# A selective-scan block on five engines: one more state's drive moved to TensorE, four of them by diagonal matrices

## The chip, the cores and the metric

One core of a Trainium2 chip runs the whole program. The metric is the device time of one execution in microseconds (us), as the median of several runs. TensorE (PE, with its weight loads PEld), VectorE (DVE), ScalarE (ACT), GpSimd (POOL) and the DMA queue of SyncE (SP) run their own instruction streams in order and wait for each other on semaphores.

## The reference

Two layers follow each other; each normalises its input over groups of 4 channels (32 groups, mean and variance over all positions) and adds its result to its input. The input is 16 images of 64 x 64 positions with 128 channels, in fp32. Layer 0 is a two-dimensional recurrent cell over rows and columns, which the change does not touch except through the shared normalisation function. Layer 1 is a bidirectional selective scan (Mamba) over the 4096 tokens of an image:

```python
def _mamba(x, in_w, conv_w, conv_b, x_w, dt_w, dt_b, A_log, D, out_w):
    xc, z = jnp.split(x @ in_w.T, 2, axis=-1)             # 256 channels each
    xc = silu(causal_conv(xc, conv_w, 4 taps) + conv_b)
    dt, Bm, Cm = jnp.split(xc @ x_w.T, [8, 8 + 16], axis=-1)
    dt = softplus(dt @ dt_w.T + dt_b)
    dA = jnp.exp(dt[..., None] * -jnp.exp(A_log))         # per channel and state
    dBx = dt[..., None] * Bm[:, :, None, :] * xc[..., None]
    h = dA_t * h + dBx_t ;  y = sum over 16 states of h * C_t
    y = (y + xc * D) * silu(z)
    return y @ out_w.T
y_fwd = _mamba(x);  y_bwd = flip(_mamba(flip(x)));  x + y_fwd + y_bwd
```

The weights are the same in both directions, so the two scans' sums can be added before the gate `silu(z)` and the output projection.

## The kernel before

Layer 1 works on an image in 16 **passes**: 8 chunks of 512 tokens forwards (the first half; passes 0 to 7), then the same 8 chunks backwards (the second half; passes 8 to 15). Channels lie on partitions in two halves (h = 0, 1) of 128, tokens on the free axis. Every pass computes for each of the 16 states s: the decay exp(dt * A) on ACT (L919), the **drive** dt * xc * B, the scan h = decay * h + drive on DVE (L952, one instruction of 128x512 for each half), the product with C, and the sum over states, which PE makes by transposing each product into an accumulating PSUM tile `py` (`sums`, L987, 8 transposes of 128x128 a state; the tile has tokens on partitions).

The states are of three kinds, and the kind says which engine does the two products:

- **plain** (7 states: 0, 6, 7, 8, 10, 12, 15): the drive on POOL (L924, `dtx` times a row of B that a DMA spread over the 128 partitions into `br`), the product with C on POOL (L978, with a row of C spread into `cr`). The decay goes into a PSUM bank.
- **mixed** (5 states: 2, 4, 5, 11, 14): the drive is made with tokens on partitions, where B is a scalar of each partition: ACT multiplies the transposed `dtxt` by it (`drive_turned`, L931, 4 instructions of 128x256), and PE transposes the result back into two PSUM banks (`drive_back`, L939, 8 transposes). The product with C stays on POOL.
- **turned** (4 states: 1, 3, 9, 13): the drive as in mixed; the scan writes in place in PSUM, the product with C is on DVE (L980), and DVE also copies the carried column (L967).

POOL makes `dtx` = dt * xc as well (L893), once a pass. Around the states stand, on PE: the convolution folded with the input projection (L801, 8 matmuls of 128x512), `xproj` (L838), `dtproj` (L876), the transposes of `dtx` (L900) and of the B columns (L858), `skip` (xc * D by a diagonal matrix into `py`, L987 with `ddiag`) and in the second half the gate's projection (L821). ACT takes most of these out of PSUM and applies silu and softplus, with three table loads a pass.

At the end of a pass, `finish`: in the first half ACT copies `py` to `yf` (L1014); in the second half DVE adds `yf` to `py` (L1017) and multiplies by the gate z into `y` (L1018). Then PE transposes `y` (`back`, L1024), ACT takes it (L1031), PE projects it with `out_wT` (`project`, L1041, 2 matmuls of 512 columns, channels on partitions), ACT copies that (`project_take`, L1052), PE transposes it to tokens on partitions (`store`, L1057, 4 transposes), and DVE adds it to the residual (L1063), which a DMA writes out.

During the first half of an image's passes the next image is read, transposed (L758), copied by ACT (L766), and its statistics are taken by DVE (L767). Then `normal` turns the statistics into scale and shift: `group_norm` averages by a matmul with `gavg` (L493), copies the mean to SBUF (L495), and DVE computes the deviation, its square and the sum with the variances (L497, L499, L500) before a second matmul (L502) and the root on ACT (L504).

The **order of the work** is not the program's nesting. `order_of_issue` lists every operation with its inputs, buffers, an assumed cost (`COST`) and an urgency (the tables `AT` and `STATE`, in units of one state); `simulate` plays them on five engines with those costs and writes down the order in which they begin. That order is fixed at build time, and each engine's queue executes its own part of it in order. `RINGS` gives the number of buffers of each kind: six PSUM banks for everything but `py` (two banks), 6 `br`, 5 `cr`, 3 `dbx`, 2 `dbt`, 3 `hst`, 4 `hc`.

```python
TURNED = (1, 3, 9, 13)
MIXED = (2, 4, 5, 11, 14)
...
# pool: plain drive                      # ACT + PE: mixed and turned drive
nc.gpsimd.tensor_mul(t, self.dtx, bc(self.brow.pop(s), 1, NH))
...
nc.scalar.activation(t[:, j, :], self.dtxt[:, j, :], AF.Copy, scale=self.bt[:, j, s : s + 1])
...
nc.tensor.transpose(t[:, j * P : (j + 1) * P], self.dbt[s][:, j, h * P : (h + 1) * P], ident)
```

Of the kernel before, what the change touches and what calls it, by code (L numbers as in the profile page):

```python
# [14 lines left out]
P = 128  # L15
# [17 lines left out]
TURNED = (1, 3, 9, 13)  # L33
MIXED = (2, 4, 5, 11, 14)
# [3 lines left out]
    "bank": 6, "py": 1, "das": 2, "dbx": 3, "dbt": 2, "hst": 3, "hc": 4,  # L38
    "br": 6, "cr": 5, "xc": 2, "dt": 2, "dtx": 2, "dtxt": 2, "dbl": 2, "bt": 2, "z": 1, "y": 1,
# [4 lines left out]
    "conv": 3.5, "gate": 0.9, "silu": 0.62, "softplus": 0.65, "gate_take": 0.6, "dtproj": 0.95,  # L44
    "xproj": 1.8, "xproj_take": 0.5, "bturn": 0.35, "bturn_take": 0.15, "times": 2.37,
    "turn": 0.55, "turn_take": 0.5, "decay": 0.62, "drive": 2.37, "drive_turned": 1.6,
    "drive_back": 0.52, "scan_turned": 1.28, "scan": 1.19, "keep_turned": 0.15, "keep": 0.1,
    "out_turned": 0.61, "out": 2.37, "sums": 1.0, "skip": 0.42, "finish": 1.0, "finish_last": 2.4,
    "back": 0.55, "back_take": 0.5, "project": 1.8, "project_take": 0.5, "store": 0.5,
    "store_take": 0.65, "residual": 0.1, "read_load": 0.1, "read_turn": 0.5, "read_take": 0.6,  # L50
    "normal": 5.0, "normalise": 0.75, "spread": 0.1, "rows": 0.1, "store_out": 0.1,
# [9 lines left out]
    "conv": -26.36,  # L61
    "gate": 4.72,
    "session": 9.0,
    "xproj": -16.72,
    "xproj_take": -15.49,
    "bturn": -16.32,
    "bturn_take": -19.05,
    "dtproj": -8.22,
    "times": -3.14,
    "turn": -1.06,  # L70
    "turn_take": -5.63,
    "skip": 5.5,
    "residual": 13.47,
    "finish": 17.28,
    "back": 19.53,
    "back_take": 20.1,
    "project": 21.46,
    "project_take": 24.04,
    "store": 24.79,
    "store_take": 25.37,  # L80
    "read_load": 1.91,
    "read_turn": 7.21,
    "read_take": 8.49,
    "normal": 2.71,
    "normalise": 1.36,
# [3 lines left out]
    "decay_turned": -0.91,  # L89
    "decay_mixed": -3.33,  # L90
    "decay_plain": -1.6,
    "drive_turned": -2.74,
    "drive_mixed": -2.49,
    "drive_back": 0.01,
    "drive": -2.5,
    "out_turned": -0.93,
    "out_mixed": 1.73,
    "out_plain": 2.27,
    "keep": -0.87,
    "sums_turned": 3.93,  # L100
    "sums_mixed": 4.73,
    "sums_plain": 6.15,
    "row_b": -6.28,
    "row_c": -4.0,
# [7 lines left out]
def order_of_issue(images):  # L112
# [5 lines left out]
    def tile_of(ring):  # L118
        tiles.append([ring, 0, None])
        return len(tiles) - 1  # L120
# [17 lines left out]
    for i in range(-2, n_pass):  # L138
# [83 lines left out]
        for s in range(NS):  # L222
# [23 lines left out]
            else:  # L246
                bt, bx = tile_of("dbt"), bank
                put("drive_turned", (s,), "ACT", at + s + STATE["drive_" + k],
                    after=[get(("turn_take", i, q)) for q in range(NB // 2)] + [get(("bturn_take", i))],
                    takes=[bt], uses=[T_["dtxt"], T_["bt"]], chain=("drive_turned", 0))  # L250
                for h in range(NH):
                    put("drive_back", (s, h), "PE", at + s + STATE["drive_back"] + 0.3 * h,
                        after=[get(("drive_turned", i, s))], takes=[bx[h]], uses=[bt],
                        chain=("bank", AHEAD))
                ready = [get(("drive_back", i, s, h)) for h in range(NH)]
            hh = bx if k == "turned" else [tile_of("hst")] * NH
            for h in range(NH):
                put("scan", (s, h), "DVE", at + s + 0.4 * h,
                    C_["scan_turned" if k == "turned" else "scan"],
# [11 lines left out]
            for h in range(NH if turned else 1):  # L271
                put("out_of", (s, h) if turned else (s,), "DVE" if turned else "POOL",
                    at + s + STATE["out_" + k] + 0.3 * h, C_["out_turned" if turned else "out"],
                    after=(scans[h : h + 1] if turned else scans) + [get(("spread", i, "c", s))],
# [11 lines left out]
        else:  # L286
            y, yt, xr = tile_of("y"), tile_of("yt"), tile_of("xr")
            put("finish", (), "DVE", at + AT["finish"], C_["finish_last"],
                after=adds + [("gate_take", i, NB // 2 - 1)], takes=[y], uses=[z])
            for h in range(NH):  # L290
# [5 lines left out]
            m, o = tile_of("misc"), tile_of("y")  # L296
            put("project", (), "PE", at + AT["project"],
                after=[get(("back_take", i, h)) for h in range(NH)], takes=[m, o], uses=[yt])
            put("project_take", (), "ACT", at + AT["project_take"], after=[get(("project", i))],
                uses=[m])  # L300
            m = tile_of("misc")
            put("store", (), "PE", at + AT["store"], after=[get(("project_take", i))], takes=[m],
                uses=[o])
            put("residual", (), "DMA", at + AT["residual"], takes=[xr])
            put("store_take", (), "DVE", at + AT["store_take"],
                after=[get(("store", i)), get(("residual", i))], uses=[m])
            put("store_out", (), "DMA", at + AT["store_take"], after=[get(("store_take", i))], uses=[xr])

        if b + 1 < images:
            if not second:  # L310
# [7 lines left out]
                    after=[get(("read_turn", b + 1, n))] + last, uses=[m])  # L318
            else:
                if n == NCH:  # L320
                    m = tile_of("misc")
                    put("normal", (), "DVE", at + AT["normal"], who=b + 1, key=("normal", b + 1),
                        after=[get(("read_take", b + 1, k)) for k in range(NCH)], takes=[m],
                        uses=[m])
# [140 lines left out]
def conv_preact_kernel(ctx: ExitStack, tc: tile.TileContext, a: dict):  # L465
# [23 lines left out]
    def group_norm(pool, psum, mv, n, tag, bank="misc"):  # L489


        pm = psum.tile([P, n], F32, name=f"pm_{tag}", tag=bank)
        nc.tensor.matmul(pm, lhsT=gavg, rhs=mv[:, :, 0], start=True, stop=True)  # L493
        mean = pool.tile([P, n], F32, name=f"mean_{tag}", tag="gn_mean")
        nc.vector.tensor_copy(mean, pm)  # L495
# [620 lines left out]
```

## Time and profile before

| what | value |
|---|---|
| median of 3 runs | 13995.0 us (13992.92 to 14003.99) |
| the profiled execution's own time | 13994.48 us |
| its span, first to last instruction | 13991.9 us |
| DVE busy | 12725.5 us, 15550 instructions |
| PE busy, PEld busy | 12411.7 us, 9345.3 us, 75020 instructions each |
| ACT busy | 12171.0 us, 22826 instructions |
| POOL busy | 12118.7 us, 5380 instructions |
| DMA | 1782.01 MB, mean 127 GB/s |

Layer 0 takes the first 1560 us or so of the span; layer 1, with 16 images of 16 passes, the rest. A group row gives line, engine, operation, the tiles (out<-in), shapes and count; then busy time, the mean length of one instruction in ns, and the idle time of the engine just ahead of them with what ended it. On PE, ACT and DVE the next instruction starts before the one ahead has ended, so the length of one (say 273 ns) is more than what a further one costs; that cost, called the **pitch** here, is the distance between starts in a timeline without idle time. A matmul of fp32 data appears as two records, a transpose as one. "Granted clock" (PEclk) is the share of full speed that TensorE was given.

### The profile page before, as it was taken

Reading aid. Unit: us, or ns where it says so; the run is one execution under the profiler, and the core shown is the slowest. Engines: PE = TensorE matmul, PEld = TensorE weight load, DVE = VectorE, ACT = ScalarE, POOL = GpSimd, SP = SyncE. Lnnn points to the kernel's source line nnn. Section 1 sums busy time; section 2 is a strip of 40 time slices with the busy share of each in tenths; the row PEclk is TensorE's granted clock in tenths of the full one; section 3 lists DMA queues with packets and bytes.
Section 4 is the critical chain, followed back from the end, with each engine's and each line's share of the span. In section 5 each row is a group of like instructions: output and inputs, shape, how many; then the busy total and the mean of one; then the engine's idle time right before and its main releaser. Section 6 shows DMA issues by size and latency. Waiting matters only on the chain. (4 is left out here: it accounts for less than half of the span.)

```text
span 13991.9 us, 233510 instructions
## 1 busy us (share of the span) xinstructions
PE 12411.7 (89%) x75020; PEld 9345.3 (67%) x75020; DVE 12725.5 (91%) x15550; ACT 12171.0 (87%) x22826; POOL 12118.7 (87%) x5380
## 2 busy tenths in 40 slices
PE   8999889898989888898989888888989898888988
PEld 7657766666666666666666666666666666666666
DVE  6777689999999999999999999999999999999998
ACT  2444699999999999999999999999999999999998
POOL 0111499999999999999999999999999999999998
PEclk7999899999999999999999999999999999999999
DMA  3221245444544545454545444454545444444544
GB/s 120 56 56 54 79 123 142 131 138 134 137 136 134 142 130 143 127 142 130 139 135 135 137 134 141 130 143 129 141 132 138 135 136 141 131 142 128 140 133 119
DMA packets 2060712, 1782.01 MB, mean 127 GB/s; under 512 B 959960, under 2 KB 1289184, under 8 KB 2059488
## 3 DMA queue, kind: packets, MB, share of 16 engines
q1 hardware_dynamic: 1981552, 1731.85, 44.2%
q10 hardware_dynamic: 77936, 35.23, 1.0%
q8 instruction: 598, 9.80, 0.3%
q14 instruction: 626, 5.13, 0.1%
HBM read 1679.37 MB, written 83.89 MB: 126 GB/s over the span
## 5 line engine op out<-in xcount | busy, mean ns | idle before, releaser
L978 POOL TENSOR_TENSOR hc<-hst,cr 128x1024 f32<-128x1024 f32 x3072 | 7228.5, 2373 | 448.0 <-DVE hst L952 245.7
L987 PE MATMUL py<-ident,hc 128*128 128x128 f32 x32768 | 4451.0, 283 | 565.8 <-POOL hc L978 449.2
L987 PEld LDWEIGHTS py<-ident,hc 128*128 128x128 f32 x32768 | 3822.0, 146 | 1328.3 <-POOL hc L978 761.1
L924 POOL TENSOR_TENSOR dbx<-dtx,br 128x1024 f32<-128x1024 f32 x1792 | 4239.8, 2377 | 1.8 <-POOL hc L978 0.4
L931 ACT ACTIVATE dbt<-dtxt,bt 128x256 f32<-128x256 f32 x9216 | 3858.4, 499 | 228.4 <-PE hps L939 226.8
L952 DVE TENSOR_TENSOR_SCAN hst<-da,carry,dbx 128x512 f32<-128x512 f32 x3136 | 3805.8, 1261 | 199.4 <-POOL dbx L924 126.6
L939 PE MATMUL hps<-ident,dbt 128*128 128x128 f32 x18432 | 2857.8, 288 | 306.8 <-ACT dbt L931 190.6
L919 ACT ACTIVATE das<-dt,A_log_sb 128x512 f32<-128x512 f32 x4608 | 3069.7, 713 | 67.3 <-DVE hps L952 43.6
L952 DVE TENSOR_TENSOR_SCAN hst<-das,carry,hps 128x512 f32<-128x512 f32 x2240 | 2727.8, 1262 | 145.8 <-issue 69.2
L939 PEld LDWEIGHTS hps<-ident,dbt 128*128 128x128 f32 x18432 | 2255.3, 148 | 731.5 <-ACT dbt L931 465.2
L919 ACT ACTIVATE da<-dt,A_log_sb 128x512 f32<-128x512 f32 x3584 | 2378.5, 682 | 106.6 <-DVE hst L952 78.4
L952 DVE TENSOR_TENSOR_SCAN hps<-das,carry,hps 128x512 f32<-128x512 f32 x1792 | 2201.4, 1269 | 149.8 <-PE hps L939 98.6
L801 PE MATMUL pp<-xT,wk 128*128 128x512 f32 x4096 | 1889.4, 604 | 120.2 <-DVE st L767 107.5
L980 DVE TENSOR_TENSOR hc<-hps,cr 128x512 f32<-128x512 f32 x2048 | 1389.7, 679 | 6.3 <-DMA cr<-rows 2.4
L621 POOL TENSOR_TENSOR a_f<-a_f,c 128x8 f32<-128x8 f32 (+31 forms) x254 | 200.0, 787 | 1354.6 <-ACT a_f L613 1179.1
L801 PEld LDWEIGHTS pp<-xT,wk 128*128 128x128 f32 x4096 | 748.5, 193 | 904.0 <-issue 765.0
L893 POOL TENSOR_TENSOR dtx<-dt,xc 128x1024 f32<-128x1024 f32 x256 | 608.1, 2376 | 52.4 <-DMA br<-rows 45.8
L876 PE MATMUL pv<-dbl,dt_wT 8*128 8x512 f32 x1024 | 530.6, 638 | 66.8 <-ACT xc L812 66.0
L952 DVE TENSOR_TENSOR_SCAN hst<-da,dbx 128x512 f32<-128x512 f32 x448 | 517.7, 1203 | 63.2 <-POOL dbx L924 53.9
L987 PEld LDWEIGHTS py<-ddiag,xc 128*128 128x128 f32 x4096 | 504.3, 192 | 59.1 <-issue 54.4
L987 PE MATMUL py<-ddiag,xc 128*128 128x128 f32 x4096 | 535.8, 275 | 2.7 <-ACT yf L1014 2.7
L838 PE MATMUL pd<-xc,x_wT_sb 128*40 128x512 f32 x1024 | 507.8, 620 | 0.0
(109 smaller groups left out, 11772.5 us busy)
## 6 DMA issues: line engine op xcount, KB each, us to landing
cr<-rows SPq DMA_DIRECT2D x4096, 256.0 KB
br<-rows SPq DMA_DIRECT2D x1792, 256.0 KB
carry<-hst SPq DMA_DIRECT2D x3072, 1.0 KB
xs<-in_x_dram SPq DMA_DIRECT2D x64, 512.0 KB
xl<-x SPq DMA_DIRECT2D x128, 256.0 KB
xr<-x SPq DMA_DIRECT2D x128, 256.0 KB
out_dram<-xr SPq DMA_DIRECT2D x128, 256.0 KB
xl<-in_x_dram SPq DMA_DIRECT2D x392, 64.0 KB
```

The source lines that it names most:

```text
L801: nc.tensor.matmul(pp, lhsT=wk[:, k, h * P : (h + 1) * P], rhs=xT[self.b % 2][:, t0 : t0 + T], start=(k == 0), stop=(k == TAPS - 1),)
L838: nc.tensor.matmul(pd, lhsT=x_wT[:, h, :], rhs=self.xc[:, h, :], start=(h == 0), stop=(h == NH - 1),)
L876: nc.tensor.matmul(pv, lhsT=dt_wT[:, h * P : (h + 1) * P], rhs=self.dbl[:RANK, :], start=True, stop=True,)
L893: nc.gpsimd.tensor_mul(self.dtx, self.dt, self.xc)
L919: nc.scalar.activation(t, self.dt[:, h, :], AF.Exp, scale=amat[:, h, s : s + 1])
L924: nc.gpsimd.tensor_mul(t, self.dtx, bc(self.brow.pop(s), 1, NH))
L931: nc.scalar.activation(t[:, j, :], self.dtxt[:, j, :], AF.Copy, scale=self.bt[:, j, s : s + 1])
L939: nc.tensor.transpose(t[:, j * P : (j + 1) * P], self.dbt[s][:, j, h * P : (h + 1) * P], ident)
L952: nc.vector.tensor_tensor_scan(t[:, self.rev], self.da.pop((s, h))[:, self.rev], dbx[:, self.rev], 0.0 if self.first else carry[:, self.d, ...
L978: nc.gpsimd.tensor_mul(self.hc[s], self.hst[s], bc(self.crow[s], 1, NH))
L980: nc.vector.tensor_mul(self.hc[s][:, h, :], self.h[s, h], self.crow[s])
L987: nc.tensor.matmul(self.py[:, j, h * P : (h + 1) * P], start=j // 2 not in self.banks, stop=self.added >= (NS + 1 - 1) * NB * NH, skip_gro ...
```

## The change

- **State kinds.** Plain states go from 7 to 6 (1, 6, 7, 10, 12, 15), mixed from 5 to 6 (0, 3, 4, 5, 11, 14); turned are four again (2, 8, 9, 13).
- **Diagonal matrices.** For four of the ten states whose drive does not come from POOL (5, 8, 11, 13), ACT builds four 128x128 diagonal matrices with B on the diagonal (`drive_diag`: the identity times a scalar of each partition), and PE multiplies `dtxt` by them, which transposes and scales at once: 8 fp32 matmuls of 128 columns instead of 8 transposes. The other six keep ACT's four instructions of 128x256 and PE's 8 transposes.
- **First direction added in PSUM.** In the second half PE adds `yf` into `py` by two identity matmuls of 512 columns (`again`); DVE's addition L1017 goes.
- **Projection with tokens on partitions.** 8 matmuls of 128 columns give the projection in the layout of the residual; ACT's copy L1052 and PE's 4 transposes L1057 go.
- **Normalisation.** `group_norm` reads the mean from PSUM, ACT squares, and the second average is made of two accumulated matmuls. `read_stats` becomes an operation of its own.
- **Rings and plan.** `br` 6 to 4 buffers, two new `dg`; `COST`, `AT` and `STATE` get new numbers throughout, so the order of all engines is a different one.

```diff
-TURNED = (1, 3, 9, 13)
-MIXED = (2, 4, 5, 11, 14)
+TURNED = (2, 8, 9, 13)
+MIXED = (0, 3, 4, 5, 11, 14)
+DIAG = (5, 8, 11, 13)
...
-    "bank": 6, "py": 1, "das": 2, "dbx": 3, "dbt": 2, "hst": 3, "hc": 4,
-    "br": 6, "cr": 5, "xc": 2, ...
+    "bank": 6, "py": 1, "das": 2, "dbx": 3, "dbt": 2, "dg": 2, "hst": 3, "hc": 4,
+    "br": 4, "cr": 5, "xc": 2, ...
...
-        mean = pool.tile([P, n], F32, name=f"mean_{tag}", tag="gn_mean")
-        nc.vector.tensor_copy(mean, pm)
+        mean, pv = pm[:, 0, :], pm[:, 1, :]
+        nc.tensor.matmul(mean, lhsT=gavg, rhs=mv[:, :, 0], start=True, stop=True)
         nc.vector.tensor_sub(dev, mv[:, :, 0], mean)
-        nc.vector.tensor_mul(sq, dev, dev)
-        nc.vector.tensor_add(sq, sq, mv[:, :, 1])
-        nc.tensor.matmul(pv, lhsT=gavg, rhs=sq, start=True, stop=True)
+        nc.scalar.activation(sq, dev, AF.Square)
+        nc.tensor.matmul(pv, lhsT=gavg, rhs=sq, start=True, stop=False)
+        nc.tensor.matmul(pv, lhsT=gavg, rhs=mv[:, :, 1], start=False, stop=True)
...
+            def drive_diag(self, s):
+                t = ring(sp, "dg", [P, NB, P], f"dg_{self.nm}_{s}")
+                for j in range(NB):
+                    nc.scalar.activation(
+                        t[:, j, :], ident, AF.Copy, scale=self.bt[:, j, s : s + 1])
+                self.dbt[s] = t
...
             def drive_back(self, s, h, place):
+                if s in DIAG:
+                    for j in range(NB):
+                        nc.tensor.matmul(
+                            t[:, j * P : (j + 1) * P],
+                            lhsT=self.dtxt[:, j, h * P : (h + 1) * P],
+                            rhs=self.dbt[s][:, j, :], start=True, stop=True)
+                    return
...
+            def again(self, j):
+                sums = yf[:, self.c * NB + 2 * j : self.c * NB + 2 * j + 2, :]
+                self.add(j, slice(None), lhsT=ident, rhs=sums.rearrange("p j d -> p (j d)"))
...
-                nc.vector.tensor_add(self.py, self.py, yf[:, sl, :])
-                nc.vector.tensor_mul(self.y, self.py, self.z)
+                nc.vector.tensor_mul(self.y, py, self.z)
...
             def project(self, place):
-                for h in range(NH):
-                    nc.tensor.matmul(po, lhsT=out_wT[:, h, :], rhs=self.yt[:, h, :], ...)
-            def project_take(self):
-                nc.scalar.copy(self.o, self.ps.pop("project"))
-            def store(self, place):
                 for j in range(NB):
-                    nc.tensor.transpose(po[:, j * P : (j + 1) * P], self.o[:, j * P : (j + 1) * P], ident)
+                    for h in range(NH):
+                        nc.tensor.matmul(po[:, j, :], lhsT=self.yt[:, h, j * P : (j + 1) * P],
+                            rhs=out_wT[:, h, :], start=(h == 0), stop=(h == NH - 1))
```

## The prediction

> **What bounds the kernel now.** I read the page first: layer 1 fills all but the first 4 of the 40 slices, and there four engines are all near nine tenths, so the shares alone name no bound.
>
> ```profile
> PE   8999889898989888898989888888989898888988
> DVE  6777689999999999999999999999999999999998
> ACT  2444699999999999999999999999999999999998
> POOL 0111499999999999999999999999999999999998
> ```
>
> So I cut stages out of the trace, each four passes long, from the end of one `finish` (L1014, L1018) to another. The first is from the last image's first half, where no next image is read; the second from a second half; the third from a first half in which the next image is read and normalised. The columns are the stretch, its length, busy time (records) of PE, PEld, DVE, ACT, POOL, the granted clock, DMA share and rate.
>
> ```profile
> 13299.50:13485.20 185.70, 159.75 (x1010) 121.00 (x1009) 172.66 (x193) 173.88 (x322) 185.70 (x81) 0.96 0.47 133
> 8291.80:8482.80 191.00, 174.27 (x1104) 132.11 (x1104) 185.28 (x204) 180.43 (x338) 186.44 (x81) 0.98 0.53 140
> 7854.40:8057.60 203.20, 168.37 (x1033) 125.64 (x1032) 186.66 (x208) 179.98 (x331) 191.19 (x83) 0.93 0.46 131
> ```
>
> An undisturbed first-half pass takes 185.7/4 = 46.4 us and POOL never pauses: it is the bound. A second-half pass takes 47.75 us, POOL 97.6% busy, DVE 97.0%. The third stretch is 17.5 us longer than the first: one normalisation. An image's period, `finish` to `finish` of two images, is 771.4 us = 8 x 46.4 + 8 x 47.75 + 18.2.
>
> For the prices I take pitches (start to next start without idle) from timelines, since busy time counts the overlapping tails:
>
> ```profile
> 8000.57 1.04 PE L987 MATMUL py<-ident,hc 128*128 128x128 f32 x8
> 8001.45 1.95 PE L987 MATMUL py<-ddiag,xc 128*128 128x128 f32 x16
> 8003.23 0.60 PE L939 MATMUL hps<-ident,dbt 128*128 128x128 f32 x4
> ...
> 8396.24 3.60 PE L801 MATMUL pp<-xT,wk 128*128 128x512 f32 x8
> 8399.68 1.03 PE L987 MATMUL py<-ident,hc 128*128 128x128 f32 x8
> ...
> 8374.72 0.20 ACT L864 COPY bt<-pbt 128x64 f32<-128x64 f32 x1
> 8374.82 0.69 ACT L919 ACTIVATE da<-dt,A_log_sb 128x512 f32<-128x512 f32 x1
> 8378.87 4.89 ACT L931 ACTIVATE dbt<-dtxt,bt 128x256 f32<-128x256 f32 x12
> ```
>
> A transpose costs (8001.45 - 8000.57)/8 = 0.11 us; a true fp32 matmul of 128 columns, `skip` with its diagonal, 1.78/8 = 0.222 (two records each); one of 512 columns 3.44/4 = 0.86. On ACT 64 columns cost 0.10, 256 with a scalar of each partition 0.40, 512 of the decay 0.61. In the same way a POOL product costs 2.32, a scan 1.175, DVE's product with C 0.60, L1017 1.26, L1018 1.14.
>
> **Floors of a pass, before.** POOL: 12 products with C, 7 drives, 1 `dtx` = 20 x 2.32 = 46.4 in both halves. DVE: 32 scans, 8 products, 8 column copies at 0.06: 42.9; with statistics 43.4 in the first half, with L1017, L1018 and the residual (0.58) 45.8 in the second. ACT: 32 decays 19.6, 36 drives 14.4, tables, silu, softplus and copies 7.9: 41.9; with L1014 and L766 43.2, with gate, `back`, L1052 and normalise 45.0. PE: 128 sums 14.0, 72 transposes 7.9, `skip` 1.8, convolution 6.9, the other projections and turns 4.6: 35.2 in the first half with nothing else, 40.0 in the second (gate 1.7, `back` 0.9, `project` and `store` 2.2).
>
> **The change part by part.**
>
> *One plain state less:* POOL does 6 drives, 19 x 2.32 = **44.1**. One DMA of 256 KB a pass goes too; `br` has 4 buffers for 6 rows instead of 6 for 7. POOL sat idle 1.8 us before L924 in the whole run, so rows come in time now; with a late row, POOL would wait, and I price that inside the overhead below.
>
> *Ten states off POOL, four by diagonals.* ACT: 24 drives of 256 columns (9.6) and 16 of 128. No row has 128 columns: between 0.10 (64) and 0.40 (256); the line through 256 (0.40) and 512 (0.61) gives 0.29, which I take as nearest in kind (SBUF source, scalar of each partition). 16 x 0.29 = 4.7; sum 14.3 against 14.4. Ends: ACT 3.0 us less or 1.7 us more; the latter would put it at 46.1 in the second half, 0.3 over PE. PE: 48 transposes (5.3) and 32 matmuls of 128 columns, which no row shows with these operands: between 0.11 (a transpose) and 0.86 (512 columns); `skip` is the same shape, type and kind, so 0.222, 7.1 in all. PE **+4.5** in every pass. The upper end would add 20 us a pass; with a row of the same shape I keep it out of the range and leave what of it is possible to the slower rival.
> The Trainium skill, "FP8 and Floating Point Precision", section "TensorE Precision Notes", says that true fp32 takes four passes through the array. If each pass cost a transpose's 0.11 us, 32 of them would cost 14.1 us, the second half would be PE-bound at over 52 us, and the kernel some 600 us slower. The row shows two records and 0.222 us for the whole product, so I go by the row.
>
> *First direction in PSUM:* DVE loses 1.26 a pass of the second half; PE gains 2 matmuls of 512 columns, 1.72. They queue behind `finish` of the pass before, as the first `sums` already do. `py` is held 1.14 us at the end instead of 2.4.
>
> *Projection:* ACT loses a copy (0.47). PE: 8 x 0.222 = 1.8 instead of 1.72 + 0.44. DVE's residual addition stays, and one PSUM bank less is taken.
>
> *More decays into SBUF* (20 instead of 18): same pitch, nothing. Carried columns by DMA, products with C, sums: same counts. The rewritten order costs nothing by itself; what it may cost is the overhead.
>
> *Normalisation.* What it stops now:
>
> ```profile
> 8026.93 7.44 DVE L497 TENSOR_TENSOR dev_l<-mv,mean_l 128x1 f32<-128x1 f32 x1
> 8039.15 2.36 POOL L978 TENSOR_TENSOR hc<-hst,cr 128x1024 f32<-128x1024 f32 x1 [4.80 <-issue]
> 8035.44 0.26 ACT L504 ACTIVATE std_l<-pv_l,eps 128x1 f32<-128x1 f32 x1 [7.37 <-PE pv_l L502]
> ```
>
> A subtraction of one column, both operands in SBUF, takes 7.44 us and ends when POOL's run of products does (8034.35); the scans, which read one operand from PSUM, keep 1.26 beside a busy POOL. From 8025.85 to 8036.01 DVE does nothing else: 10.2 us. After, the mean is read from PSUM, so I price the subtraction at 0.16 and the chain at 0.35 + 0.54 + 0.16 + square, table load and root on ACT (about 2.1) + 0.4 = 3.6 us. ACT's own stop goes from 10.2 to about 3. Of 18.2 us between 6.6 (the stop alone) and 11.7 (in proportion) go; I take 9, leaving 9. Ends: 0 and 18.2 left.
>
> **Sum.** Floors after: first half POOL 44.1, DVE 43.4, ACT 43.1, PE 39.7 (40.2 with reading); second half **PE 45.8**, DVE 44.5, ACT 44.4, POOL 44.1. What lies above the floor depends on how close the second engine is: before, 0 where the next stood at 93.5% (first half) and 1.35 us = 2.9% where it stood at 98.7% (second half). After, the second engine stands at 98.4% and 97.2%, so I take 2.9% twice: 45.4 and 47.1. An image: 8 x 45.4 + 8 x 47.1 + 9 = 749 against 771.4, 22.4 less; 15 images give 336, the last (no normalisation) 8 x 1.0 + 8 x 0.65 = 13, and the last pass's tail about 1. 13994.5 - 350 = 13644, say **13640** (the profiled execution's own time, 0.5 below the median, so it stands for it).
>
> **Rivals.**
>
> *The floors are reached* (1% above them, 44.5 and 46.3, 6.5 us left of the normalisation): 733 an image, -39 x 15 - 27 = 13390. For it: POOL ran at 100% for four passes. Against: never with three others within 4%. 15%.
>
> *TensorE becomes the bound of the second half and gives its gain back there* (47.75 stays, 45.4 in the first half, 9 left): 754 an image, -17 x 15 - 8, 13730. For it: its floor rises from 40.0 to 45.8. Against: it is often ahead of its inputs. 20%.
>
> *Slower: TensorE starves in its own queue.* Its order is fixed; each of 10 drives and 16 sums waits on ACT, POOL or a PSUM bank, and the matmuls behind wait too. Today 7.75 us of a second-half pass are not used by its pitches (47.75 - 40.0), most because nothing is asked of it. If 6 of them are stops that stay, a pass is 51.8: 8 x 51.8 + 8 x 45.4 + 9 = 787, +15 x 15 + 24, 14250. It decides from 45.8 + 4.1 = 49.9 on, where the second half loses the 8 + 9 us that the rest of the image gains. 10%.
>
> *It doesn't unload what bounds:* the other engines, at 43 to 45 us, hold passes where they are, and only the normalisation gains: -9 x 15, 13860. Against: first-half passes with POOL at 100%. 5%.
>
> **How the numbers follow.** Forecast 50%, rivals 15, 20, 10, 5. Range: 1% above the floors gives 13390; 5% above them (46.3, 48.1) with 11.6 left gives 767, -4.4 x 15, some 13920. About two in ten lie outside: part of the first rival below, the third above. A measurement of this kernel tells about 0.2% (28 us) from no change: faster 86%, same 3%, slower 11%.
>
> **What would show it.** POOL's L924 at 1536 instead of 1792, idle time on POOL in both halves. PE's busy time in a second-half pass over 46 us of some 47, the diagonal products at a pitch of 0.22, and DVE and POOL waiting for PE there. First-half passes near 45.4. ACT's 128-column products at 0.29. DVE's deviation at 0.16, and a stop of 3 to 4 us. Wrong would be: diagonal products at 0.4 or more, POOL late for `br` rows, second-half passes over 48 us.

## The result, and the profile after

| what | before | after |
|---|---|---|
| median of 4 runs each, same chip | 13995.2 us (13992.9 to 14004.0) | 14081.9 us (14072.0 to 14086.9) |
| profiled execution, its span | 13994.5, 13991.9 us | 14082.9, 14081.1 us |
| mean granted clock of the execution | 0.956 | 0.982 |

The changed kernel is **slower**, by little: the ratio of the times is 1.006, with an interval of 1.0043 to 1.0077, or 87 us. Forecast were 13640 us, in a range of 13390 to 13920.

The page of the changed kernel, busy shares by slice:

```profile
PE   8999899999999999999999999999999999999999
DVE  6777689898989989898989989898989999998998
ACT  2444699999999999999989999999989999999998
POOL 0111499899989999899999999899989999999998
```

Before, POOL and DVE were at nine tenths in every slice of layer 1; now both drop to eight in slices that come back about every 2.2 slices, which is an image (781 us of 352 us slices). Something that happens once an image has become longer. The last slices, with the last image, hardly show it.

Stretches cut where `finish` begins (L1050 first half, L1053 second half; the prediction's stretches are cut there too, not at its end), columns as in the prediction (length; PE, PEld, DVE, ACT, POOL busy; clock; DMA). The first holds four first-half passes of the last image, during which no image is read; the second four second-half passes; the third the passes in which the next image is read, from the first `finish` of an image to its ninth (seven first-half passes and the first of the second half):

```profile
13407.10:13588.20 181.10, 169.58 (x1166) 134.49 (x1167) 173.58 (x192) 173.19 (x337) 176.11 (x77) 0.99 0.46 130
8348.00:8538.50 190.50, 188.66 (x1314) 152.93 (x1314) 180.27 (x201) 179.16 (x350) 177.33 (x77) 1.00 0.50 135
7903.80:8299.20 395.40, 359.82 (x2385) 281.40 (x2383) 345.84 (x391) 358.46 (x686) 351.06 (x151) 0.97 0.43 124
```

Undisturbed first-half passes take 45.3 us here and 44.9 us in most of that image (before 46.4). Second-half passes take 47.6 (before 47.75); PE is 99% busy. Passes with reading take 395.4/8 = 49.4, with no engine above 91%: five engines wait for one another. Their intervals are 52.8, 45.4, 48.3, 48.1, 49.4, 48.1, 51.5 and 51.9 us.

This image therefore takes 8 x 44.9 + 8 x 47.6 + 41.6 = 781.6 us, where the forecast had 8 x 45.4 + 8 x 47.1 + 9 = 749. The two halves came out as forecast to within 0.5 us a pass, with opposite signs. **The remainder, what an image takes beyond its undisturbed passes, is 41.6 where 9 was written.** From the first `finish` of the first image to that of the last, 15 images later, after takes 110.8 us more than before (779.8 an image against 772.4); from there to the end it takes 17.7 us less, since nothing is read.

The prices of the new instructions, in timelines of the changed kernel (start, length, engine and line; x16 is 16 records):

```profile
8652.07 1.95 PE L955 MATMUL hps<-dg,dtxt 128*128 128x128 f32 x16
8653.85 0.60 PE L964 MATMUL hps<-ident,dbt 128*128 128x128 f32 x4
...
8678.06 1.26 ACT L945 ACTIVATE dg<-ident,bt 128x128 f32<-128x128 f32 x4
8679.23 0.67 ACT L924 ACTIVATE da<-dt,A_log_sb 128x512 f32<-128x512 f32 x1
...
8235.32 0.36 DVE L776 BATCH_NORM_AGGREGATE mv<-st 128x2 f32<-128x48 f32 x1
8236.22 0.16 DVE L502 TENSOR_TENSOR dev_l<-mv,pm_l 128x1 f32<-128x1 f32 x1 [0.54 <-PE pm_l L500]
8238.22 0.16 DVE L510 RECIPROCAL scale_l<-std_l 128x1 f32<-128x1 f32 x1 [1.84 <-ACT std_l L508]
8238.42 0.16 DVE L512 SCALAR_TENSOR_TENSOR shift_l<-pm_l,scale_l 128x1 f32<-128x1 f32 x1
```

From start to start, 8 products with a diagonal matrix take 8653.85 - 8652.07 = 1.78, or 0.222 each; four products of 128 columns on ACT 1.17, or 0.29 each; the deviation takes 0.16, and DVE's stop for the normalisation is 8238.5 - 8235.3 = 3.2 us. All four are what the prediction wrote (0.222, 0.29, 0.16, 3.6).

POOL's groups (line, tiles, count; busy, mean ns; idle time ahead and what ended it), first the product with C before the change, then the drive and the product with C after it:

```profile
L978 POOL TENSOR_TENSOR hc<-hst,cr 128x1024 f32<-128x1024 f32 x3072 | 7228.5, 2373 | 448.0 <-DVE hst L952 245.7
...
L929 POOL TENSOR_TENSOR dbx<-dtx,br 128x1024 f32<-128x1024 f32 x1536 | 3639.8, 2373 | 8.6 <-DVE hst L976 5.4
L1002 POOL TENSOR_TENSOR hc<-hst,cr 128x1024 f32<-128x1024 f32 x3072 | 7235.0, 2371 | 877.3 <-DVE hst L976 690.7
```

POOL makes 1536 drives, as forecast, and is never late for rows of B (8.6 us in the whole run). But ahead of the products with C it now stands idle for 877 us, 691 of them ended by a scan; before, it was 448. POOL was relieved, and what it gained it spends waiting.

### The profile page after: what moved, and what is told of

Its sections match the earlier page's. It is cut to its first block, busy times and chain, and to the rows that moved or that the text cites. A ratio compares the mean times of both kernels' runs of the same rounds, so it can differ in the third digit from the quotient of the medians.

```text
span 14081.1 us, 256078 instructions
## 1 busy us (share of the span) xinstructions
PE 13269.0 (94%) x86830; PEld 10456.2 (74%) x86830; DVE 12459.2 (88%) x15371; ACT 12154.2 (86%) x23739; POOL 11552.9 (82%) x5124
## 5 line engine op out<-in xcount | busy, mean ns | idle before, releaser
L929 POOL TENSOR_TENSOR dbx<-dtx,br 128x1024 f32<-128x1024 f32 x1536 | 3639.8, 2373 | 8.6 <-DVE hst L976 5.4
L924 ACT ACTIVATE das<-dt,A_log_sb 128x512 f32<-128x512 f32 x5120 | 3431.4, 712 | 192.1 <-DVE hps L976 109.5
L976 DVE TENSOR_TENSOR_SCAN hst<-da,carry,dbx 128x512 f32<-128x512 f32 x2688 | 3301.1, 1266 | 192.7 <-ACT da L924 173.9
L976 DVE TENSOR_TENSOR_SCAN hst<-das,carry,hps 128x512 f32<-128x512 f32 x2688 | 3326.3, 1265 | 160.5 <-PE hps L955 83.3
L936 ACT ACTIVATE dbt<-dtxt,bt 128x256 f32<-128x256 f32 x6144 | 2607.3, 498 | 89.7 <-PE hps L964 76.7
L955 PEld LDWEIGHTS hps<-dg,dtxt 128*128 128x128 f32 x16384 | 2006.2, 194 | 322.8 <-issue 157.0
L955 PE MATMUL hps<-dg,dtxt 128*128 128x128 f32 x16384 | 2133.4, 279 | 58.6 <-DVE hst L976 55.3
L964 PE MATMUL hps<-ident,dbt 128*128 128x128 f32 x12288 | 1867.1, 280 | 288.6 <-DVE hst L976 139.7
L964 PEld LDWEIGHTS hps<-ident,dbt 128*128 128x128 f32 x12288 | 1406.4, 142 | 799.9 <-issue 314.5
L945 ACT ACTIVATE dg<-ident,bt 128x128 f32<-128x128 f32 x4096 | 1300.8, 392 | 164.9 <-PE hps L955 164.7
```

What stands on the lines that cost most here:

```text
L924: nc.scalar.activation(t, self.dt[:, h, :], AF.Exp, scale=amat[:, h, s : s + 1])
L945: nc.scalar.activation(t[:, j, :], ident, AF.Copy, scale=self.bt[:, j, s : s + 1])
L955: nc.tensor.matmul(t[:, j * P : (j + 1) * P], lhsT=self.dtxt[:, j, h * P : (h + 1) * P], rhs=self.dbt[s][:, j, :], start=True, stop=True,)
L976: nc.vector.tensor_tensor_scan(t[:, self.rev], self.da.pop((s, h))[:, self.rev], dbx[:, self.rev], 0.0 if self.first else carry[:, self.d, ...
```

## The experiments

Three theories could make the 32 us an image that are missing. **Order:** the new plan places the reading of the next image badly (the order is made at build time around a PSUM bank that is taken early and given back late), and all engines pay for it in every first half. **TensorE:** PE, 99% busy in the second half and raised in the first, is the bound, and reading comes on top. **Normalisation:** the new `group_norm` costs more in its place than the old one.

Runs e2 to e10 and e12 have one execution each, and the chips differ: the kernel before took between 13988.8 and 14004.0 us in all its executions, so differences of some 15 us between runs say nothing.

What the order has to do with a bank: `read_turn` (L762) writes the transposed part of the next image into one of six PSUM banks, and the bank is free again after `read_take` (L767) and the statistics (L772). One such bank in the trace of after, instructions of tile `pt` with first and last start:

```profile
L762 PE MATMUL pt<-ident,xl x4: 273/273/273, 8666.4 to 8666.7; 128*128 128x128 f32 x4
L772 DVE BATCH_NORM_STATS2 st<-pt x1: 698/698/698, 8687.4 to 8687.4; 128x6 f32<-128x512 f32 x1
L767 ACT COPY xT<-pt x1: 563/563/563, 8692.3 to 8692.3; 128x512 f32<-128x512 f32 x1
```

The bank is held for 26 us of a pass of some 50, for work of 1.7 us. From the first transpose's start to the end of the last instruction that reads the tile, the mean over images 2 to 16 is 25.7 us, before the change 21.5.

### The bank held shortly (e1_hold)

```diff
-    "read_turn": -1.87, "read_take": 10.56,
+    "read_turn": 30.0,  "read_take": -100.0,
```

> The changed kernel with two numbers of its urgency table changed: the copy and the statistics of a tile read for the next image are due at once (read_take 10.56 to -100), its transposes late (read_turn -1.87 to 30), so that the tile stays in its PSUM bank for about 1 us instead of 26. The work is the same, the order is made anew from these numbers. Theory 'bank' (reading the next image costs some 40 us an image because its tile sits in one of the two banks that the order leaves for everything but decays and drives): first-half passes fall from 49.4 to about 46, an image from 781.6 to about 750, 13600 to 13700 us in all. Rival 'TensorE' (its load is too high with the diagonal products, reading only adds to it) and rival 'normalisation' (the stop between statistics and scale): neither sees a reason for a change; 14030 to 14130.

Measured **13730.6 us** (13724.7 to 13741.9, 4 runs), before 13994.1; ratio 0.9814 (0.9797 to 0.9830). The same tile in eight passes of this kernel, starts of the transposes, statistics and copies close together:

```profile
L762 PE MATMUL pt<-ident,xl x32: 272/273/327, 7715.9 to 7893.6; 128*128 128x128 f32 x32
L772 DVE BATCH_NORM_STATS2 st<-pt x8: 690/699/701, 7716.6 to 7894.6; 128x6 f32<-128x512 f32 x8
L767 ACT COPY xT<-pt x8: 566/586/590, 7717.7 to 7894.0; 128x512 f32<-128x512 f32 x8
```

The mean hold is 2.2 us. The time lies 31 us above what theory "bank" allowed and far below its rivals' 14030. Two numbers of the plan turn a loss of 87 us into a gain of 263, with the same instructions. The second half stays at 47.6 us a pass; all of it comes from the passes with reading, 378.7 us for the same eight passes instead of 395.4.

### No reading at all, in both kernels (e2_noread, e3_before_noread)

Images 1 to 15 compute on the first image's input; nothing is read, transposed or normalised for them, and each kernel's order is made anew without these operations.

```diff
-        if b + 1 < images:
+        if False:
...
-                        rhs=xT[self.b % 2][:, t0 : t0 + T],
+                        rhs=xT[0][:, t0 : t0 + T],
```

> The changed kernel without reading: images 1 to 15 use image 0's normalised input, so loads, transposes, copies, statistics and normalisation of 15 images are left out, from the order too. Theory 'bank' and rival 'normalisation' alike: all first halves run like the last image's (44.9 a pass), second halves stay at 47.6; 740 to 745 us an image, 13450 to 13520 in all. Rival 'TensorE': its 0.4 us of transposes a pass is all that is saved, first-half passes stay above 48; 13950 to 14050.

> The kernel before without reading, in the same way. Its image takes 771.4 us and its undisturbed passes 46.4 and 47.75, so reading should cost it 17 to 18 us an image: 13995 - 15 x 17.8 = 13730, whichever theory holds. Beside the run without reading of the changed kernel this says what the change is worth where no next image is read: some 230 us by the last image's passes.

Measured 13515.5 and **13727.6 us**, before (whole) 13994.1 on the same chip. So reading costs the changed kernel 14081.9 - 13515.5 = 566 us, 37.8 an image, and the kernel before 266 us, 17.8 an image. Without reading the change gains 212 us. The same eight passes of e2:

```profile
7603.30:7967.20 363.90, 342.68 (x2353) 271.73 (x2352) 345.96 (x385) 347.52 (x674) 353.98 (x153) 0.99 0.46 130
```

45.5 us a pass, and POOL 97% busy: there the forecast of 45.4 holds.

### The order kept, the reading's bodies skipped (e12_skip_reading)

The order is that of after, made around the reading, but the reading's operations issue nothing; images compute on the first one's input, as in e2.

```diff
-                if name in whole:
-                    whole[name](who, *args)
-                else:
+                if name not in whole:
```

> The changed kernel with its order of everything else kept as the plan wrote it around the reading, but nothing of the reading done: loads, transposes, copies, statistics and normalisation of images 1 to 15 are left out, and all images use image 0's normalised input. If the bank is what costs at run time (others wait for it to be released), first-half passes fall to 45 as in the run with a plan without reading: 13515. If the cost was written into the order (each queue in turn waits for an order that was made round the held bank), little is gained: 13900 to 14080.

Measured **13962.4 us**, before 13988.8. Of the 566 us that e2 gained, e12 gains 120; **447 us are paid by an order made around work that is no longer there.** Its passes (the same eight, then four of the second half):

```profile
7852.60:8237.80 385.20, 352.08 (x2355) 271.92 (x2353) 341.14 (x380) 346.05 (x667) 350.61 (x151) 0.99 0.43 123
8334.20:8525.00 190.80, 188.85 (x1313) 152.88 (x1314) 180.18 (x200) 179.25 (x349) 177.40 (x77) 1.00 0.48 135
```

The eight passes take 385.2 us against 363.9 in e2, with nothing read in either. No instruction of the reading runs, and DVE does not stop for a normalisation. This parts the order from the work: the theory of the order stands. The plan fixes for every tile which PSUM bank it gets, too, and e12 keeps that: the bank set aside for a read tile stays unused there. So "order" means the sequence together with the banks, and e12 does not part these two.

One piece of it can be seen. In after and in e12 the two halves of the convolution are issued back to back, as one block of 7 us, in four passes of each image; in e9 and e10 (below) in about one, in e1, e2, e11 (below) and before the change in none. In after (PE's timeline, then those of ACT and DVE; idle time ahead and its releaser in brackets):

```profile
8645.20 7.04 PE L806 MATMUL pp<-xT,wk 128*128 128x512 f32 x16
...
8650.17 0.69 ACT L817 ACTIVATE xc<-pp,conv_b_sb 128x512 f32<-128x512 f32 x1
...
8653.16 3.45 DVE L976 TENSOR_TENSOR_SCAN hps<-das,hps 128x512 f32<-128x512 f32 x3 [2.28 <-PE hps L955]
...
8654.05 1.28 ACT L945 ACTIVATE dg<-ident,bt 128x128 f32<-128x128 f32 x4 [3.19 <-PE hps L955]
```

The diagonal products (L955) stand behind 7 us of convolution in PE's queue; DVE waits 2.28 us for them and ACT 3.19. If every such wait lengthened its pass in full, 4 x 3.2 = 13 us of the 37.8 an image would lie in such blocks (an estimate from this one). The rest is spread over many waits that the trace shows but that no run here priced one by one.

### Other holds of the bank (e9_take_only, e10_long_hold, e8_before_hold)

e9 is after with `read_take` at -100 alone; e10 is after with `read_turn` at 30 and `read_take` at 40; e8 is the kernel before with e1's two numbers.

```diff
# e9
-    "read_take": 10.56,
+    "read_take": -100.0,
# e10
-    "read_turn": -1.87, "read_take": 10.56,
+    "read_turn": 30.0,  "read_take": 40.0,
# e8, in the kernel before
-    "read_turn": 7.21, "read_take": 8.49,
+    "read_turn": 30.0, "read_take": -100.0,
```

> The changed kernel with one number changed (read_take 10.56 to -100): the bank is held about 1 us, and the order is another than both the changed kernel's and the first experiment's. Theory 'bank': most of the gain of the first experiment, 13700 to 13830. Rival 'the first experiment's order is better by luck': any time, as likely near 14080.

> The changed kernel with read_turn at 30 as in the first experiment, but read_take at 40, so that the bank is held some 23 us again; once more another order. Theory 'bank': the gain of the first experiment is gone, 14000 to 14300. Rival 'moving the transposes late is what gained': 13700 to 13800.

> The kernel before with the two numbers of the first experiment (read_take to -100, read_turn to 30), so that a tile read for the next image sits in its PSUM bank for about 1 us; order made anew. If the held bank costs any kernel of this kind the same, 15 x 23 us less: 13650. If it costs only where the passes are not bound by GpSimd: within 100 us of 13995, since first-half passes stay at 46.4 and what reading costs is mostly the normalisation stop.

| kernel | mean hold of the bank, us | time, us | before on that chip |
|---|---|---|---|
| after | 25.7 | 14081.9 | 13995.2 |
| e10_long_hold | 20.8 | 14004.6 | 13997.0 |
| e9_take_only | 2.1 | 13879.6 | 13997.0 |
| e1_hold | 2.2 | 13730.6 | 13994.1 |
| before | 21.5 | 13995.2 | |
| e8_before_hold | 2.9 | 14016.7 | 13990.3 |

Among these orders of after, those with a short hold are faster than those with a long one. But the hold is not the whole: e9 and e1 hold the bank equally long and differ by 149 us, with `read_turn` at another place, and the expectation of e9 was missed by 50 us; e10 came out at the edge of what the bank theory had said (14000). The fastest order of all, e11 below, holds it for 8.5 us. Before the change, a short hold gains nothing (e8 is 26 us slower): in that kernel POOL sets the pace of the first half, and the re-made order lost on two passes of 54.6 and 52.6 us. What these runs show is that moving the reading's place in the plan moves the time by 350 us; that the held bank is the reason in each case is not shown.

### TensorE's work taken out (e4_no_again, e5_diag_as_transpose)

e4 leaves out the addition of the first direction in the second half (two matmuls of 512 columns, 1.72 us of PE a pass); e5 transposes `dtxt` without multiplying by B where after multiplies by a diagonal matrix (3.6 us of PE less in every pass). Both keep the order of after.

```diff
# e4, in again
-                self.add(j, slice(None), lhsT=ident, rhs=sums.rearrange("p j d -> p (j d)"))
+                pass
# e5, in drive_back
-                        nc.tensor.matmul(t[...], lhsT=self.dtxt[...], rhs=self.dbt[s][:, j, :], ...)
+                        nc.tensor.transpose(t[...], self.dtxt[...], ident)
```

> The changed kernel in the same order with the two identity matmuls of the second half left out, so that the first direction's sums are missing from the output. Theory 'TensorE bounds the second half' (busy 99% there, 47.6 us a pass): 1.72 us a pass go, passes near 46, 8 x 16 x 1.6 = 205 us in all, 13870 to 13890. Rival 'the order as a whole bounds it, TensorE only fills its waits': passes stay within 0.5 us of 47.6, 14020 to 14080.

> The changed kernel in the same order; PE transposes the unscaled product instead of multiplying it by the diagonal matrix, so the factor B is left out for four states and the 32 fp32 matmuls of a pass (0.222 us) become 32 transposes (0.11). ACT still builds the diagonals, but no longer waits for PE to have read them. PE does 3.6 us a pass less; by the chain traced back through second-half passes about half of these products lie on the loop that sets the pass, by the one through first-half passes some two thirds. Theory 'loop' (what lies on the loop TensorE - ScalarE - VectorE of a pass counts, `again` lay off it): second half 47.6 to 45.8, first half some 2.5 us less, 13500 to 13650 in all. Rival 'TensorE only fills its waits': like the run without the identity matmuls, under 50 us.

Measured 14066.4 (before 13994.1) and 13857.1 (before 13990.3). Four second-half passes of e4, then of e5:

```profile
8392.60:8583.00 190.40, 184.38 (x1297) 149.95 (x1298) 180.16 (x200) 179.04 (x349) 177.44 (x77) 1.00 0.49 135
```

```profile
8280.20:8468.10 187.90, 179.31 (x1185) 137.59 (x1185) 179.78 (x200) 178.15 (x349) 177.39 (x77) 1.00 0.52 136
```

In e4, PE's busy time falls by 4.3 us in four passes, and the passes stay at 47.6. In e5 it falls by 9.4 and they go to 47.0. An engine that is 99% busy was thus not the bound by its load. What bounds instead was only traced: I followed the second half of after back by hand through two passes, and a loop of 47.6 us runs from DVE's `y` (L1053, which frees the only `py`) over PE's sums, `skip`, convolution, half of the diagonal products, gate and `dtproj` (some 35 us), ACT's softplus, decays and drives (some 10 us), a scan and PE's last sums, to the next `y`. `again` lies beside ACT's part of it, which agrees with e4. The loop alone would have brought e5's passes to 45.8; they stay at 47.0, with DVE 95.7% and POOL 94.4% busy, and what sets these 47.0 is not shown. With 3.6 us of PE less in all 256 passes, 922 us of PE's work, e5 gains 225, between what its two theories had said (some 430 to 580, and under 50).

### The normalisation alone (e6_old_norm, e7_before_new_norm)

e6 is after, same order, with the old `group_norm`; e7 is before, same order, with the new one.

```diff
# e7 (e6 is the reverse)
...
-        mean = pool.tile([P, n], F32, name=f"mean_{tag}", tag="gn_mean")
-        nc.vector.tensor_copy(mean, pm)
+        mean, pv = pm[:, 0, :], pm[:, 1, :]
...
-        nc.vector.tensor_mul(sq, dev, dev)
-        nc.vector.tensor_add(sq, sq, mv[:, :, 1])
+        nc.scalar.activation(sq, dev, AF.Square)
...
```

> The changed kernel in the same order with group_norm as it was before (mean copied to SBUF, square and sum on VectorE). If the normalisation edit gains what was forecast (9 of 18 us an image), 15 x 9 = 135 us are lost: 14220. If the stop of 10 us was hidden by buffers or by other waits: 14080 to 14120.

> The kernel before in its own order with the changed group_norm alone. Forecast of the edit: 15 x 9 = 135 us less, 13860, between 13995 - 15 x 6.6 = 13896 and 13995 - 15 x 11.7 = 13820. If the stop is hidden: 13960 to 14000.

e7 takes **13846.4 us** (before 13990.3): 144 us less, 9.6 an image, where the prediction took 9. e6 takes 14100.8 (before 13990.3), only 19 us more than after (24 when each is taken against before on its chip). DVE's timeline of e6 around a normalisation:

```profile
8255.29 0.36 DVE L778 BATCH_NORM_AGGREGATE mv<-st 128x2 f32<-128x48 f32 x1
8256.19 0.16 DVE L501 COPY mean_l<-pm_l 128x1 f32<-128x1 f32 x1 [0.54 <-PE pm_l L499]
8256.38 0.74 DVE L503 TENSOR_TENSOR dev_l<-mv,mean_l 128x1 f32<-128x1 f32 x1
8257.15 2.26 DVE L505 TENSOR_TENSOR sq_l<-dev_l 128x1 f32<-128x1 f32 x1
8259.45 0.16 DVE L506 TENSOR_TENSOR sq_l<-sq_l,mv 128x1 f32<-128x1 f32 x1
...
8260.86 2.46 DVE L978 TENSOR_TENSOR_SCAN hst<-da,carry,dbx 128x512 f32<-128x512 f32 x2
```

The old chain stops DVE for 5.6 us here, not for 10.2: the subtraction takes 0.74 instead of 7.44, and the square 2.26. Both end where a product of POOL does (two products run from 8254.75 to 8259.40), and then POOL itself waits 4.15 us for its next input; before, the subtraction outlasted three products, from 8027.43 to 8034.35. Undoing the edit adds 2.4 us of stop an image and 1.2 to 1.6 us of time. The edit is worth 9.6 us an image in one order and 1.2 to 1.6 in the other, which is hardly more than the noise.

### After's operations in another order (e11_replanned)

All urgencies found anew by a search over the kernel's own plan, with PE's assumed costs raised by 0.008 us each; what is computed is unchanged.

```diff
-    "conv": -26.66, "gate": 1.7, "dtproj": -13.06, ...
+    "conv": -27.76, "gate": 3.93, "dtproj": -16.19, ...
-    "read_turn": -1.87, "read_take": 10.56, "normalise": 5.24,
+    "read_turn": -2.33, "read_take": 3.12, "normalise": 65.22,
```

> The changed kernel with urgencies found by a search over the plan, in which every operation of TensorE costs 0.008 us more than its pitches (for the change from one group to the next); the operations are the same. In the plan, first-half passes with reading take 44.6 and second-half ones 47.2. Theory 'order' (the change pays where the order does not lose it again): first half near 45.5, second 47.6, 13530 to 13650. Rival 'the four engines are too full for any order': not under the first experiment's 13730.

Measured **13646.2 us** (13644.1 to 13649.7, 4 runs), before 13997.0; ratio 0.9749 (0.9733 to 0.9765). It is the fastest full kernel here, 351 us faster than before. Eight passes with reading, and four of the second half:

```profile
7692.90:8059.80 366.90, 346.77 (x2376) 274.04 (x2377) 347.10 (x395) 353.41 (x682) 351.64 (x152) 0.99 0.47 131
8156.00:8345.60 189.60, 187.63 (x1314) 152.60 (x1313) 180.46 (x200) 179.43 (x349) 177.81 (x77) 1.00 0.50 136
```

Passes with reading take 45.9 us instead of 49.4; the second half 47.4. The bank is held 8.5 us. That this lies by the forecast of 13640 shows that these operations can run in that time; it does not make the forecast right, which was for another order.

## Why the prediction was wrong, point by point

- **POOL's floor and the first half: right.** 19 products a pass, 44.9 us undisturbed where 45.4 was forecast, rows of B never late.
- **The diagonal products: right.** 0.222 us on PE and 0.29 on ACT. The Trainium skill ("FP8 and Floating Point Precision", "TensorE Precision Notes") speaks of four passes for true fp32; the product of 128 columns shows two records and twice a transpose's 0.11 us, as `skip` had before.
- **The second half: right within 0.5 us a pass** (47.6 for 47.1), and the reason half wrong. The rival "TensorE becomes the bound of the second half and gives its gain back there" had the length (47.75), but taking work off PE in e4 moved nothing: it is not PE's load. That a chain through PE, ACT and DVE in their fixed order bounds instead is argued from the trace.
- **The normalisation's price: right in the kernel before** (9.6 us an image in e7 for the 9 taken) and its stop right in the kernel after (3.2 for 3.6).
- **The step that failed** is "The rewritten order costs nothing by itself; what it may cost is the overhead", together with "Of 18.2 us between 6.6 (the stop alone) and 11.7 (in proportion) go; I take 9, leaving 9". The prediction took the whole of an image's excess before for one normalisation, because a stop of 10.2 us was plain to see in it. Reading in fact costs 17.8 us an image before (e3), of which the new normalisation takes away 9.6 (e7); the remaining 8 are the reading's own work and its place in the order. In the new order reading costs 37.8 us an image (e2): (566 - 447)/15 = 8 for its execution, the new normalisation included, and 447/15 = 29.8 for the order made around it (e12). In the old order the 9 would have come out, 17.8 - 9.6 = 8.2; the rewritten order, which was put at nothing, is what made it 41.6 in an image's sum.
- **The range** was worked out with 6.5 and 11.6 us left of this term, inside the ends of 0 and 18.2 that were named for it. Both suppose that a rewritten plan cannot make an image's excess larger than it was, and no row of the trace of before could have said otherwise. The kernel itself could: `simulate`, run to the end, gives the plan's own time of an image, 768 us for after and 774 for before (means of 15 images). By its own clock the new plan gained 6 us an image, where the forecast had 22. (The sum of the first rival, from which the lower end comes, gives 13382 as written, not 13390; nothing rests on it.)
- **The slower rival** had the sign and not the place: it put the loss into the second half (51.8 a pass; measured 47.6), and what lengthened were first-half passes with reading. That engines stop because a fixed queue has the wrong thing in front (convolution ahead of diagonal products) is its mechanism, elsewhere and in part only.

What the plan's own clock shows, with its assumed costs, against the image's time as measured (first `finish` to first `finish`, means of 15 images):

| order | plan, us | measured, us |
|---|---|---|
| after | 768 | 779.8 |
| e10_long_hold | 767 | 774.1 |
| e9_take_only | 752 | 766.4 |
| e1_hold | 744 | 756.0 |
| e11_replanned | 742 | 751.6 |
| e2_noread | 736 | 742.1 |

It ranks the orders of after as the chip does, and it sees the fault: reading costs after 768 - 736 = 32 us an image in the plan, and before 774 - 768 (e3) = 6. When `simulate` is given a seventh bank for the read tiles alone, it still counts 761 for after, and 769 for e1's numbers. By this clock, then, the held bank is a small part of the fault, and a free bank alone does not bring e1's gain; no run here tried it on the chip.

What stays open: which waits of the new order make up the 30 us an image, beyond the convolution blocks, and why this search over urgencies ended at such an order.

## What to carry to other kernels

Where the order of all queues is fixed at build time, every edit of costs or urgencies is a change of the whole order, and it deserves a term of its own in the sum with bounds on both sides; where the program has a clock of its own for that order, read it for both kernels before forecasting. Price an excess by taking its parts out one at a time: removing the loudest stop in it (10.2 us here) can be worth half of it or, in another order, almost nothing. And a busy share of 99% does not make an engine the bound; work taken off it and a time that stays the same show that it isn't.

## What the runs showed of the hardware

TensorE runs at half its speed for some microseconds after some stops. In PE's timeline of after, the same product `skip` of 16 records, once after a short wait and once after two waits of 2.45 and 0.70 us with little between them:

```profile
8634.82 2.05 PE L1011 MATMUL py<-ddiag,xc 128*128 128x128 f32 x16 [0.88 <-DVE y L1053]
...
8685.15 0.63 PE L964 MATMUL hps<-ident,dbt 128*128 128x128 f32 x4 [2.45 <-DVE carry L991]
8686.48 3.68 PE L1011 MATMUL py<-ddiag,xc 128*128 128x128 f32 x16 [0.70 <-ACT yf L1050]
8690.00 0.60 PE L964 MATMUL hps<-ident,dbt 128*128 128x128 f32 x4
```

The second one takes 8690.00 - 8686.48 = 3.52 us to the next start, the first one 1.89 (the next starts at 8636.71). So waits of some 3 us cost TensorE about 1.6 more; the granted clock from 8686.48 to 8690.00 is 0.52, from 8634.80 to 8636.70 it is 1.00. It is 0.97 over the passes with reading and 1.00 in the second half. No run here took such a stop away by itself.

The same happens without any stop. Here PE is never idle, and yet the granted clock goes from 1.00 to 0.50 at 5734:

```profile
5730.51 1.12 PE L881 MATMUL pv<-dbl,dt_wT 8*128 8x512 f32 x2
5731.56 1.09 PE L1011 MATMUL py<-ident,hc 128*128 128x128 f32 x8
5732.59 1.12 PE L881 MATMUL pv<-dbl,dt_wT 8*128 8x512 f32 x2
5733.64 0.82 PE L964 MATMUL hps<-ident,dbt 128*128 128x128 f32 x4
5734.25 1.92 PE L1011 MATMUL py<-ident,hc 128*128 128x128 f32 x8
5735.96 1.75 PE L955 MATMUL hps<-dg,dtxt 128*128 128x128 f32 x8
```

Eight transposes take 1.71 us to the next start instead of 0.88 or so. Ahead of them stand the matmuls of `dtproj` (L881), with 8 rows instead of 128. Layer 1 of after can be cut into 3550 stretches of 3.41 us, the length of most of its half-clock stretches; in 2833 of them PE is busy for over 90%. `dtproj` takes over 60% of 32 of these, and 31 of the 32 are followed by half clock; of the other 2801 none is (in e11, cut in the same way, 19 of 20 and none). Transposes do not slow it: in 108 of the 2801 they take almost all of PE's time. So in this kernel a busy TensorE is slowed, too, where most of its time goes to matmuls with few rows.

How long a DVE subtraction of one column with both operands in SBUF takes depends on POOL's products beside it: 7.43 to 7.47 us through three of them in 14 of the 15 normalisations of the kernel before, 0.73 to 0.99 to the end of the first of two in 14 of the 15 of e6, and 0.15 or 0.16 in after, beside a busy POOL, with one operand in PSUM. Why it waits for three products in one case and for one in the other is open.
